# Nineteen block products instead of twenty-one in a per-sample weight combination, and a new order of one iteration

## The chip, the cores and the metric

The kernel runs on one core of a Trainium2 chip. The metric is the device time of one execution in microseconds (us), the smaller the better. The kernel before takes 482.57 us, the median of three runs (482.04 to 482.87).

## The reference

The input is x (128 samples, 64 channels, 1024 positions, float32) and a style vector of 128 numbers for each sample. Four convolutions of width 3 follow one another, of the kinds same, upsample, same, downsample. Each sample has its own weights: the shared ones, multiplied by a scale for each input channel that comes from the style, and normalised for each output channel. The upsample and the downsample have a fixed blur [1, 3, 3, 1]. No nonlinearity stands between the layers.

```python
def _layer(x, style, w, b, mw, mb, typ):
    s = style @ mw.T + mb
    weight = SCALE * w * s[:, None, :, None]
    demod = lax.rsqrt(jnp.sum(weight * weight, axis=(2, 3)) + EPS)
    weight = weight * demod[:, :, None, None]
    if typ == 'same':
        out = jax.vmap(_conv_same)(x, weight) + b[None, :, None]
    elif typ == 'upsample':
        out = jax.vmap(_conv_up)(x, weight.transpose(0, 2, 1, 3)) + b[None, :, None]
        out = _blur(out, 2.0 * blur_k, (1, 1))
    elif typ == 'downsample':
        xb = _blur(x, blur_k, (2, 2))
        out = jax.vmap(_conv_down)(xb, weight) + b[None, :, None]
...
out = x
for i, typ in enumerate(('same', 'upsample', 'same', 'downsample')):
    out = _layer(out, style, weights[i], biases[i], mod_w[i], mod_b[i], typ)
return x + out
```

## The kernel before, in words

Since everything is linear, the kernel folds the four layers and the two blurs into one convolution for each sample, and applies that one to x. The rows near the two ends of the sequence don't fit the folded convolution; they are worked out apart for all samples at once (functions `ends0` to `ends3` and `rest0` to `rest3_bias`), a small step in some of the iterations, and leave in a transfer of their own (`out_ends`).

**Tiling.** Four samples form a quad; there are 32 quads (`NQ`). Two samples stand above one another in the 128 partitions (64 channels each), and the other two beside them. Every matmul is therefore a 64 x 64 tile of TensorE, and four of them (rows upper or lower, columns upper or lower) make one step. The profile counts two TensorE instructions for each float32 matmul of the code.

**Weights of a quad, in three combinations.** All products here are of blocks, 64 x 64 numbers for each sample. `scale3` makes the scaled weights of the last layer (`wd`). `stage1` (for most quads in two halves, `stage1_a` and `stage1_b`) multiplies in layer 2 and leaves `S`. `stage2` multiplies in the upsampling layer and the blurs and leaves `R`, seven blocks for each sample, called r0 to r6 here. For most quads a part of `stage2` is worked out an iteration early (`share`, which writes into free columns of the bank of a running convolution, and `share_copy`, which ScalarE copies over). `stage3` multiplies in layer 0 and leaves the folded weights `Wf`: three kinds of output position, three blocks each. Kind 0 uses the plain weights w, kind 1 w/3, kind 2 -2w (`w0s`). `stage3` is called in two parts: kinds 0 and 1 into one pair of PSUM banks, kind 2 into the same pair afterwards, each followed by two scaled copies on ScalarE into `Wf`. With three weight taps and seven blocks a kind takes seven block products, so the three kinds take 21.

**The convolution of a quad.** The three kinds are combined on VectorE into five sets of weights (`combine_a`, `combine_b`; tile `H`, which with `Wf` serves five products) and x into five inputs (`in04`, `in1`, `in2`, `in3`, tile `T`). `conv3`, `conv1`, `conv2`, `conv4` and `conv0` are the five products, each in three groups of 340 columns; conv4 writes to `Y`, the others to `psA`. `sum1` and `sum2` on VectorE put the results together, `output` on ScalarE scales them and adds the bias, and `store` sends them out.

**Order.** Nothing is scheduled by a planner: the kernel switches to manual scheduling, and each engine takes its instructions in the order in which the Python code writes them. The loop over q (line 1207) overlaps five quads. In iteration q it does, for TensorE: `stage2` of c = q+2, `conv4` of q, `stage3` part 0 of c, `conv3` of n = q+1, `stage3` part 1 of c, group 0 of `conv0` of q, group 0 of `conv1` of n, `stage1_a` of s = q+4, the other two groups of `conv1`, group 1 of `conv0`, `stage1_b`, `share`, group 2 of `conv0`, and `conv2` of n. The steps of the row ends stand in `EXTRA` and `SLOTS`, by iteration and place. Waits between engines are put in by the framework where one instruction touches a tile that another engine reads or writes.

**PSUM.** The pool `ps_w` has one pair of banks, used in turn by `psS`, `psR`, `psW` and, for the row ends, `psE`; `ps_conv` has two pairs for `psA`, `ps_y` one for `Y`.

Of the kernel before, what the change touches and what calls it, by code (L numbers as in the profile page):

```python
# [48 lines left out]
F32 = mybir.dt.float32  # L49
# [5 lines left out]
C = 64  # L55
K = 3
# [7 lines left out]
def kernel(  # L64
# [9 lines left out]
    nc = tc.nc  # L74
    NP, P, NXC = x.shape
    B = 2 * NP
    NQ = B // 4
# [3 lines left out]
    HALF = (T, Bo)  # L81

    nc_v, nc_a, nc_g = nc.vector, nc.scalar, nc.gpsimd
# [3 lines left out]
    const = ctx.enter_context(tc.tile_pool(name="const", bufs=1))  # L87
    setup = ctx.enter_context(tc.tile_pool(name="setup", bufs=2))
    wd_pool = ctx.enter_context(tc.tile_pool(name="wd_pool", bufs=4))
    s_pool = ctx.enter_context(tc.tile_pool(name="s_pool", bufs=4))  # L90
    r_pool = ctx.enter_context(tc.tile_pool(name="r_pool", bufs=4))
    wf_pool = ctx.enter_context(tc.tile_pool(name="wf_pool", bufs=3))
    tpool = ctx.enter_context(tc.tile_pool(name="tpool", bufs=2))
    mpool = ctx.enter_context(tc.tile_pool(name="mpool", bufs=1))
# [3 lines left out]
    ps_w = ctx.enter_context(tc.tile_pool(name="ps_w", bufs=1, space=PSUM))  # L98
# [35 lines left out]
    woi = {2: weights(cuts[1] + KC), 0: weights(cuts[2] + 2 * KC), 1: weights(cuts[2] + 3 * KC)}  # L134
# [12 lines left out]

    one = const.tile([P, 1], F32, name="one")
    eps = const.tile([P, 1], F32, name="eps")
    Z = const.tile([P, 512], F32, name="Z")  # L150
    E = const.tile([P, NT, C], F32, name="E")
    w1s = const.tile([P, K + 1, K, C], F32, name="w1s")
    nc_v.memset(one, 1.0)
# [40 lines left out]
    wsq = const.tile([P, NL, K, C], F32, name="wsq")  # L194
# [70 lines left out]
    def var_newton(bs, ls=slice(0, NL)):  # L265
# [90 lines left out]
    Wq = {}  # L356
    chain = {}

    def scaled_copy(eng, dst, src, f):
        if eng is nc_a:  # L360
            nc_a.activation(dst, src, AF.Copy, scale=f)  # L361
        else:
            eng.tensor_scalar(dst, src, f, None, op0=ALU.mult)
# [39 lines left out]
    def flat(t):  # L403
        return t.rearrange("c a o -> c (a o)")
# [43 lines left out]
        whole[q] = t  # L448

    whole, shared_ps = {}, {}  # L450
    Ed = const.tile([P, 6, C], F32, name="Ed")

    def tap_differences():

# [66 lines left out]
    def stage2(q, pool=None, engs=(nc_a, nc_a), between=None):  # L521
        st = chain[q]
        shared = q in shared_ps
        ps = stage2_rest(q) if shared else unit(pool or ps_w, f"psR{q}")
        for n, e in enumerate(() if shared else (-2, -1, 0, 1, 2, 3, 4, 5, 6)):
            if e % 2 == 0:
                a, lo, m = slice(1, 4), e // 2 + 1, 3
            else:
                a, lo, m = slice(4, 6), (e + 3) // 2, 2
            for r, rows in enumerate(HALF):  # L530
                for c, cols in enumerate(HALF):
                    src = st[c if r == 0 else 1 - c]
# [10 lines left out]
        rt = []  # L543
        for r in range(2):
            t = r_pool.tile([P, 7, C], F32, tag="R", name=f"R{q}_{r}")
            scaled_copy(
                engs[r], t.rearrange("c t o -> c (t o)"), ps[r][:, : 7 * C], tC[:, q, r : r + 1]
            )
            rt.append(t)
        chain[q] = rt  # L550
        return ps

    def stage3(q, part, pool=None, engs=(nc_a, nc_a)):

        rt = chain[q]
        ps = unit(pool or ps_w, f"psW{q}_{part}")
        if part == 0:
            Wq[q] = (
                wf_pool.tile([P, 2, K, K, C], F32, tag="Wf", name=f"Wf{q}"),
                wf_pool.tile([P, 3, 2, K, C], F32, tag="H", name=f"H{q}"),  # L560
            )
        W = Wq[q][0]
        kinds = ((0, 1), (2,))[part]
        n = 0
        for i, kind in enumerate(kinds):
            for k in range(K):
                gs = [g for g in range(K) if 0 <= K * g + kind - k < 7]
                lo, m = gs[0], len(gs)
                first = K * lo + kind - k
                n += 1  # L570
                for r, rows in enumerate(HALF):
                    for c, cols in enumerate(HALF):
                        at = (K * i + lo) * C
                        nc.tensor.matmul(  # L574
                            ps[r][cols, at : at + m * C],
                            w0s[kind][rows, k, :],
                            rt[c][rows, first : first + K * (m - 1) + 1 : K, :],
                            start=(n == 1),
                            stop=(n == K * len(kinds)),
                            skip_group_check=True,  # L580
                        )
        for r in range(2):
            dst = W[:, r, kinds[0] : kinds[-1] + 1].rearrange("c t g o -> c (t g o)")
            scaled_copy(engs[r], dst, ps[r][:, : len(kinds) * K * C], t0[:, q, r : r + 1])
        return ps

    def residual(q):

        W = Wq[q][0]
        for r in range(2):  # L590
            v = W[:, r, 1, 1, :]
# [4 lines left out]

    def taps(q):
        W, H_ = Wq[q]
        return *(W[:, :, i] for i in range(K)), *(H_[:, i] for i in range(3))

    def combine_a(q):

# [71 lines left out]
    def product(q, m, ps, groups=range(K)):  # L674

        W, H_ = Wq[q]
        tag, i = SLOT[m]
        for g in groups:
            for s, rows in enumerate(HALF):
                for c, cols in enumerate(HALF):  # L680
                    if m in (0, 4):
                        w = W[rows, c, m // 2, g, :]
                    else:
                        w = H_[rows, m - 1, c, g, :]
                    nc.tensor.matmul(  # L685
                        ps[s][cols, :NB],
                        w,
                        Ts[q, tag][rows, c, i, g : g + NB],
                        start=(g == 0 and m == 3),
                        stop=(g == K - 1),  # L690
                        skip_group_check=True,
                    )
# [26 lines left out]
    def conv1(q, *groups):  # L719
        product(q, 1, banks(q), groups or range(K))  # L720
# [19 lines left out]
    def conv0(q, *groups):  # L740
        product(q, 0, banks(q), groups)
# [294 lines left out]
    first = PART[0]  # L1036
# [125 lines left out]


    EXTRA = {
        (1, 1): lambda: small_rest(1),
        (2, 1): lambda: (small_rest(2), var_root(REST, Y[:, 0])),
        (2, 2): lambda: (table_B(REST), table_Bn(REST), vector_a1(REST)),
        (3, 0): lambda: var_newton(*layers(2, 3)),
# [20 lines left out]
        (22, 0): lambda: (blur_side(0, 0), blur_side(1, 0)),  # L1189
        (23, 0): lambda: (blur_side(0, 1), blur_side(1, 1)),  # L1190
        (24, 0): lambda: (blur_side(0, 2), blur_side(1, 2)),
        (28, 1): rest3,
        (28, 2): rest3_bias,
    }

    def extra(*at):
# [6 lines left out]

    def late(q):
        return AHEAD <= q < NQ - 2

    for q in range(NQ):
        n, c, s = q + 1, q + 2, q + 3 + (q >= AHEAD)
# [20 lines left out]
        if n < NQ - 1:  # L1229
            if q == 0:  # L1230
                in_g01(n)
            if q == 1:
                in_g2(n)
                load(n + NX)
            combine_a(n)
            combine_b(n)
            if q == 0:
                in_g2(n)
                load(n + NX)
# [38 lines left out]
        if late(q):  # L1278
            for i in range(2):
                store(q, i, slice(2, K))  # L1280
            if late(q - 1):
                for i in range(3):
                    load(c + 1, slice(i, i + 1))
        if c < NQ:
            stage3(c, 0)
        conv3(n)
        copy_m3(n)
# [3 lines left out]
        if q in SMALL:  # L1291
            l, bs = SMALL[q]
# [3 lines left out]
            in3(c)  # L1296
        if q > 1:
            in_g01(c)
        if c < NQ:
            stage3(c, 1)  # L1300
        if q in SLOTS:
            slot(*SLOTS[q], Y_banks)
        if s < NQ:
            conv0(q, 0)
        if q in SMALL:
            small(q)
        if q == 2:
# [144 lines left out]
```

## Time and profile before

| | us |
|---|---|
| median of three runs | 482.57 |
| the profiled execution | 482.28 |
| its span, first to last instruction | 480.4 |
| TensorE busy | 472.2 (98%) |
| VectorE busy | 399.0 (83%) |
| ScalarE busy | 303.8 (63%) |
| one iteration of the steady middle (349.47 to 363.41) | 13.94 |

The profile is of one execution. PE is TensorE, PEld its weight loads, DVE VectorE, ACT ScalarE, POOL GpSimd, SP the queue that issues most transfers. A row of the groups names line, engine and operation, then output tile and inputs, shapes and count; behind the bars stand busy time, mean length of one, and the engine's idle time ahead of them with what ended it. A row of the timeline gives start, length, and how many instructions were merged into it, with idle time ahead of it in brackets. In the chain of waits a step of TensorE begins where the step before it ended. Line 685 is the matmul of the convolutions, 574 that of `stage3`, 467 those of `share` and the remaining `stage2`, 533 the full `stage2`, 390 `stage1`; line 361 holds all scaled copies on ScalarE, line 753 the outputs.

### The profile page before, as it was taken

What the parts mean: (1) busy time and instruction counts of PE and PEld (TensorE: products, weight loads), DVE (VectorE), ACT (ScalarE), POOL (GpSimd) and SP (SyncE); (2) the same over time, 40 slices, a digit from 0 to 9 for tenths busy, and PEclk for the clock granted to TensorE, in tenths of its full rate; (3) what the DMA queues carried; (4) which work ended last, traced back from release to release, by engine and by line L of the source; (5) the groups of instructions that cost most, each with busy time, mean ns of one, the idle gap of its engine ahead of it and who ended that gap; (6) DMA issues with size and microseconds to landing.
All of it is one profiled execution on the core that took longest, in us unless ns stands there. A gap on an engine that the chain in (4) does not pass through costs nothing.

```text
span 480.4 us, 25778 instructions
## 1 busy us (share of the span) xinstructions
PE 472.2 (98%) x11592; PEld 369.2 (77%) x11592; DVE 399.0 (83%) x660; ACT 303.8 (63%) x620; POOL 138.9 (29%) x171
## 2 busy tenths in 40 slices
PE   8999999999999999999999999999999999999995
PEld 7977787888788777878777798767777887877762
DVE  4899998799898888878868898758988887777984
ACT  5466666666667666766666666667666666665442
POOL 2533032635413333302333212333112333322100
PEclk9999999999999999999999999999999999999998
DMA  7116364245555346544445545345544445554314
GB/s 243 53 63 194 118 195 191 92 149 172 164 159 149 115 138 180 163 136 140 141 137 178 150 150 145 125 148 161 165 142 129 151 150 180 169 157 151 106 60 175
DMA packets 50494, 70.65 MB, mean 147 GB/s; under 512 B 5648, under 2 KB 47312, under 8 KB 50384
## 3 DMA queue, kind: packets, MB, share of 16 engines
q1 hardware_dynamic: 49792, 68.32, 44.7%
q8 instruction: 91, 1.49, 1.3%
q10 hardware_dynamic: 592, 0.69, 0.4%
q14 instruction: 19, 0.16, 0.1%
HBM read 35.36 MB, written 33.62 MB: 144 GB/s over the span
## 4 chain that ended last, share of the span: by engine, by line
PE 97%; DVE 2%; issue 0%; ACT 0%; ACTq 0%; DVEq 0%
PE psA L685 45%; PE psW L574 15%; PE Y L685 11%; PE psR L467 10%; PE psS L390 6%; PE psR L533 4%; PE psA L467 2%; PE Y L921 2%; PE Y L337 1%; PE Y L181 1%; DVE Oe L1011 0%; PE psM L205 0%; DVE o L755 0%; DVE y L595 0%; PE psE L921 0%
## 5 line engine op out<-in xcount | busy, mean ns | idle before, releaser
L685 PE MATMUL psA<-T,H 64*64 64x340 f32 x2304 | 193.3, 446 | 1.2 <-DVE y L595 0.9
L685 PEld LDWEIGHTS psA<-T,H 64*64 64x64 f32 x2304 | 100.2, 133 | 46.6 <-issue 3.3
L446 POOL TENSOR_TENSOR S<-S 128x128 f32<-128x128 f32 x28 | 15.0, 536 | 268.7 <-ACT S L361 261.5
L595 DVE SCALAR_TENSOR_TENSOR G<-X 128x684 f32<-128x684 f32 (+1 forms) x65 | 76.2, 1207 | 0.0
L685 PE MATMUL psA<-T,Wf 64*64 64x340 f32 x768 | 74.8, 446 | 0.0
L361 ACT ACTIVATE R<-psR,tC 128x448 f32<-128x448 f32 x63 | 36.5, 630 | 43.4 <-PE psR L467 26.8
L361 ACT ACTIVATE Wf<-psW,t 128x384 f32<-128x384 f32 (+1 forms) x126 | 56.3, 497 | 11.1 <-PE psW L574 10.8
L685 PE MATMUL Y<-T,Wf 64*64 64x340 f32 x768 | 62.9, 447 | 0.2 <-issue 0.2
L574 PE MATMUL psW<-R,w0s 64*64 64x128 f32 (+1 forms) x1536 | 63.1, 287 | 0.0
L574 PEld LDWEIGHTS psW<-R,w0s 64*64 64x64 f32 x1536 | 53.2, 133 | 5.9
L595 DVE SCALAR_TENSOR_TENSOR Y<-m,psA 128x680 f32<-128x680 f32 x32 | 27.8, 870 | 33.3 <-PE psA L685 33.3
L663 POOL TENSOR_TENSOR T<-G 128x684 f32<-128x684 f32 x28 | 50.9, 1817 | 0.0
L467 PE MATMUL psR<-S,E 64*64 64x64 f32 (+1 forms) x1536 | 50.6, 237 | 0.2 <-issue 0.2
L672 DVE TENSOR_TENSOR T<-G 128x1368 f32<-128x1368 f32 (+1 forms) x33 | 50.6, 1536 | 0.0
L658 POOL TENSOR_TENSOR T<-G 128x684 f32<-128x684 f32 x28 | 46.5, 1660 | 13.1 <-DVE G L595 13.1
L753 ACT ACTIVATE o<-Y,tb,td 128x340 f32<-128x340 f32 x63 | 36.6, 630 | 19.3 <-PE Y L685 16.7
L467 PEld LDWEIGHTS psR<-S,E 64*64 64x64 f32 x1536 | 43.2, 134 | 5.1 <-issue 0.3
L595 DVE SCALAR_TENSOR_TENSOR y<-psA,m 128x680 f32<-128x680 f32 x32 | 27.7, 865 | 23.1 <-PE psA L685 20.6
L390 PEld LDWEIGHTS psS<-wd,w2n 64*64 64x64 f32 x1120 | 38.3, 133 | 9.5
L685 PEld LDWEIGHTS Y<-T,Wf 64*64 64x64 f32 x768 | 32.9, 133 | 13.9 <-issue 1.1
L753 ACT ACTIVATE o<-psA,tb,td 128x340 f32<-128x340 f32 x63 | 37.0, 644 | 8.0 <-PE psA L685 8.0
L361 ACT ACTIVATE S<-psS,tBn 128x256 f32<-128x256 f32 x56 | 23.5, 470 | 28.2 <-PE psS L390 28.2
(153 smaller groups left out, 703.6 us busy)
## 6 DMA issues: line engine op xcount, KB each, us to landing
out<-o SPq DMA_DIRECT2D x167, 170.0 KB, 2.7
X<-in_x SPq DMA_DIRECT2D x150, 172.0 KB, 3.5
X<-in_x SPq DMA_DIRECT2D x14, 516.0 KB, 4.9
out<-o SPq DMA_DIRECT2D x6, 510.0 KB, 5.6
out<-o SPq DMA_DIRECT2D x2, 340.0 KB, 2.7
Xe<-in_x_ends SPq DMA_DIRECT2D x1, 512.0 KB, 6.5
out<-o ACTq DMA_DIRECT2D x3, 170.0 KB, 3.1
par<-in_params SPq DMA_DIRECT2D x2, 192.0 KB, 3.3
```

Source lines behind the costliest of these rows:

```text
L361: nc_a.activation(dst, src, AF.Copy, scale=f)
L390: nc.tensor.matmul(ps[r][cols, at * C : (at + n) * C], weight[rows], wd[c if r == 0 else 1 - c][rows, taps], start=first, stop=last, skip_ ...
L446: nc_g.tensor_add(t[:, :, 2], t[:, :, 2], t[:, :, 0])
L467: nc.tensor.matmul(dst[r][cols], weight[rows], st[c if r == 0 else 1 - c][rows, slots, :], start=False, stop=last, skip_group_check=True,)
L533: nc.tensor.matmul(ps[r][cols, lo * C : (lo + m) * C], E[rows, e + 2, :], src[rows, a, :], start=(n == 0), stop=(n == 8), skip_group_check ...
L574: nc.tensor.matmul(ps[r][cols, at : at + m * C], w0s[kind][rows, k, :], rt[c][rows, first : first + K * (m - 1) + 1 : K, :], start=(n == 1 ...
L595: nc_v.scalar_tensor_tensor(out, x, f, y, op0=ALU.mult, op1=op)
L658: eng.tensor_add(t[:, :, 0, :NJ], plane(g, 2), plane(g, 1))
L663: eng.tensor_sub(t[:, :, 1, :NJ], plane(g, 2), plane(g, 1))
L672: nc_v.tensor_sub(t[:, pairs, :, :NJ], both(a, PL), both(b, 1))
L685: nc.tensor.matmul(ps[s][cols, :NB], w, Ts[q, tag][rows, c, i, g : g + NB], start=(g == 0 and m == 3), stop=(g == K - 1), skip_group_check ...
L753: nc_a.activation(dst, src, AF.Identity, bias=add, scale=d3)
```

## The change

From quad 4 on (c = 4 to 31, 28 quads, the test `wide(q)`) the third combination is written anew. Kind 0 needs w0·r3 + w1·r2 + w2·r1 and kind 1 needs, over three, w0·r4 + w1·r3 + w2·r2 (and the same three blocks further on). Both hold w1 times one of two neighbours. With p = w1·(r2 + r3), kind 0 becomes p + w2·r1 + (w0 - w1)·r3 and kind 1 becomes p/3 + (w0/3)·r4 + ((w2 - w1)/3)·r2. So p is multiplied once and used twice; that takes 19 block products.

The new pieces: `r_sums` on VectorE makes the two sums and keeps them in `R`, whose tile grows from seven to nine blocks and holds both samples' halves; `tap_shares` on GpSimd makes the two weight differences, once; `stage3_b` does kind 2 and the first block of kind 0; `stage3_p` does p, and ScalarE writes p/3 from PSUM to PSUM beside it; `stage3_a` adds the rest. In `Wf` the kinds stand in another order (`KIND`), so that each of the two results is one run of blocks.

The order of a wide iteration changes too: `stage3_b` and `stage3_p` stand where part 0 stood, group 0 of `conv0` goes ahead of `stage3_a`, the three groups of `conv1` stand together ahead of `stage1_a`, and groups 1 and 2 of `conv0` together ahead of `stage1_b`. The two last steps of the row ends are called later, `rest3` at place 2 of iteration 28 and `rest3_bias` at place 0 of iteration 29. The weight differences `Ed` and `Wd` take over the space of `wsq`, and the constant `Z` has 384 columns.

```diff
-    r_pool = ctx.enter_context(tc.tile_pool(name="r_pool", bufs=4))
+    r_pool = ctx.enter_context(tc.tile_pool(name="r_pool", bufs=2))
-    Z = const.tile([P, 512], F32, name="Z")
+    Z = const.tile([P, 384], F32, name="Z")
-    Ed = const.tile([P, 6, C], F32, name="Ed")
+    later = wsq.rearrange("c l k o -> c (l k) o")
+    Ed = later[:, :6]
...
+    def tap_shares():
+        nc_g.tensor_sub(Wd[:, 0], woi[0][:, 0, :], woi[0][:, 1, :])
+        nc_g.tensor_sub(Wd[:, 1], w0s[1][:, 2, :], w0s[1][:, 1, :])
...
+    def same_row(ps, at, n, weight, t, slots, first=False, last=False):
+        for r, rows in enumerate(HALF):
+            for c, cols in enumerate(HALF):
+                nc.tensor.matmul(
+                    ps[r][cols, at * C : (at + n) * C],
+                    weight[rows],
+                    t[rows, c, slots, :],
+                    start=first,
+                    stop=last,
+                    skip_group_check=True,
+                )
...
+    def r_sums(q):
+        t = chain[q]
+        nc_v.tensor_add(t[:, :, 7:9], t[:, :, 2:6:3], t[:, :, 3:7:3])
+
+    def stage3_out(q, ps, at, i, j):
+        W = Wq[q][0]
+        for r in range(2):
+            dst = W[:, r].rearrange("c t g o -> c (t g) o")[:, i:j]
             scaled_copy(
+                nc_a, flat(dst), ps[r][:, at * C : (at + j - i) * C], t0[:, q, r : r + 1]
             )
+
+    def stage3_b(q):
+
+        new_w(q)
+        t = chain[q]
+        ps = wide_ps[q] = unit(ps_w, f"psW{q}")
+        same_row(ps, 3, 3, w0s[2][:, 2, :], t, slice(0, 7, 3), first=True)
+        same_row(ps, 3, 2, w0s[2][:, 1, :], t, slice(1, 5, 3))
+        same_row(ps, 3, 2, w0s[2][:, 0, :], t, slice(2, 6, 3))
+        same_row(ps, 6, 1, w0s[0][:, 0, :], t, slice(0, 1), last=True)
+        stage3_out(q, ps, 3, 0, 4)
+
+    def stage3_p(q):
+
+        ps, t = wide_ps[q], chain[q]
+        same_row(ps, 0, 2, w0s[0][:, 1, :], t, slice(7, 9))
+        for r in range(2):
+            scaled_copy(nc_a, ps[r][:, 3 * C : 5 * C], ps[r][:, : 2 * C], 1.0 / 3.0)
+
+    def stage3_a(q):
+
+        ps, t = wide_ps.pop(q), chain[q]
+        same_row(ps, 2, 2, w0s[1][:, 0, :], t, slice(1, 5, 3))
+        same_row(ps, 2, 1, w0s[1][:, 1, :], t, slice(0, 1))
+        same_row(ps, 0, 2, w0s[0][:, 2, :], t, slice(1, 5, 3))
+        same_row(ps, 0, 2, Wd[:, 0], t, slice(3, 7, 3))
+        same_row(ps, 3, 2, Wd[:, 1], t, slice(2, 6, 3), last=True)
+        stage3_out(q, ps, 0, 4, 9)
...
-        (28, 1): rest3,
-        (28, 2): rest3_bias,
+        (28, 2): rest3,
+        (29, 0): rest3_bias,
...
+    def wide(q):
+        return 2 <= q < NQ - 2
...
-            combine_b(n)
+            if wide(q):
+                combine_b(n, (0,))
+                r_sums(c)
+                combine_b(n, (1, 2))
+            else:
+                combine_b(n)
...
-        if c < NQ:
+        if wide(q):
+            stage3_b(c)
+            stage3_p(c)
+        else:
             stage3(c, 0)
         conv3(n)
...
-        if c < NQ:
+        if wide(q):
+            conv0(q, 0)
+            stage3_a(c)
+        else:
             stage3(c, 1)
         if q in SLOTS:
             slot(*SLOTS[q], Y_banks)
-        if s < NQ:
+        if not wide(q):
             conv0(q, 0)
...
-        conv1(n, 0)
+        conv1(n, *(range(K) if wide(q) else (0,)))
         if twice:
             stage1(s - 1)
         elif s < NQ:
             stage1_a(s)
         elif q == NQ - 4:
             slot(ends3, 3, unit(ps_w, "psE"), 3)
-        conv1(n, 1, 2)
+        if not wide(q):
+            conv1(n, 1, 2)
...
-        conv0(q, *((1,) if s < NQ else (0, 1)))
+        conv0(q, *((1, 2) if wide(q) else (1,)))
...
-        conv0(q, 2)
+        if not wide(q):
+            conv0(q, 2)
```

More of the change, by code (lines that the diff above doesn't have):

```diff
@@ L542, in stage2 @@
             between()
-        rt = []
+        t = r_pool.tile([P, 2, 9, C], F32, tag="R", name=f"R{q}")
         for r in range(2):
-            t = r_pool.tile([P, 7, C], F32, tag="R", name=f"R{q}_{r}")
+            scaled_copy(engs[r], flat(t[:, r, :7]), ps[r][:, : 7 * C], tC[:, q, r : r + 1])
+        chain[q] = t
+        return ps
+    KIND = {0: 1, 1: 2, 2: 0}
+    Wd = later[:, 6:8]
+    def tap_shares():
+        nc_g.tensor_sub(Wd[:, 0], woi[0][:, 0, :], woi[0][:, 1, :])
+        nc_g.tensor_sub(Wd[:, 1], w0s[1][:, 2, :], w0s[1][:, 1, :])
@@ new lines, in new_w @@
+    def new_w(q):
+        Wq[q] = (
+            wf_pool.tile([P, 2, K, K, C], F32, tag="Wf", name=f"Wf{q}"),
+            wf_pool.tile([P, 3, 2, K, C], F32, tag="H", name=f"H{q}"),
+        )
[9 more added lines that the diff above has]
+                    skip_group_check=True,
+                )
@@ L546, in stage2 @@
+    wide_ps = {}
+    def r_sums(q):
[5 more added lines that the diff above has]
+            dst = W[:, r].rearrange("c t g o -> c (t g) o")[:, i:j]
             scaled_copy(
-                engs[r], t.rearrange("c t o -> c (t o)"), ps[r][:, : 7 * C], tC[:, q, r : r + 1]
+                nc_a, flat(dst), ps[r][:, at * C : (at + j - i) * C], t0[:, q, r : r + 1]
@@ L548, in stage2 @@
             )
-            rt.append(t)
-        chain[q] = rt
-        return ps
+    def stage3_b(q):
[7 more added lines that the diff above has]
+        stage3_out(q, ps, 3, 0, 4)
@@ L557, in stage3 @@
         if part == 0:
[L558 to L561, printed above, removed]
+            new_w(q)
         W = Wq[q][0]
@@ L576, in stage3 @@
                             w0s[kind][rows, k, :],
-                            rt[c][rows, first : first + K * (m - 1) + 1 : K, :],
+                            rt[rows, c, first : first + K * (m - 1) + 1 : K, :],
                             start=(n == 1),
@@ L582, in stage3 @@
         for r in range(2):
-            dst = W[:, r, kinds[0] : kinds[-1] + 1].rearrange("c t g o -> c (t g o)")
+            at = KIND[kinds[0]]
+            dst = W[:, r, at : at + len(kinds)].rearrange("c t g o -> c (t g o)")
             scaled_copy(engs[r], dst, ps[r][:, : len(kinds) * K * C], t0[:, q, r : r + 1])
@@ L590, in residual @@
         for r in range(2):
-            v = W[:, r, 1, 1, :]
+            v = W[:, r, KIND[1], 1, :]
             nc_v.scalar_tensor_tensor(v, idn3, t3[:, q, r : r + 1], v, op0=ALU.mult, op1=ALU.add)
@@ L598, in taps @@
         W, H_ = Wq[q]
-        return *(W[:, :, i] for i in range(K)), *(H_[:, i] for i in range(3))
+        return *(W[:, :, KIND[i]] for i in range(K)), *(H_[:, i] for i in range(3))
     def combine_a(q):
@@ L681, in product @@
                     if m in (0, 4):
-                        w = W[rows, c, m // 2, g, :]
+                        w = W[rows, c, KIND[m // 2], g, :]
                     else:
@@ L1164 @@
     EXTRA = {
-        (1, 1): lambda: small_rest(1),
+        (1, 1): lambda: (small_rest(1), tap_shares()),
         (2, 1): lambda: (small_rest(2), var_root(REST, Y[:, 0])),
```

## The prediction

> **What bounds the kernel now.** I read the page first: shares, slices, chain.
>
> ```profile
> span 480.4 us, 25778 instructions
> PE 472.2 (98%) x11592; PEld 369.2 (77%) x11592; DVE 399.0 (83%) x660; ACT 303.8 (63%) x620; POOL 138.9 (29%) x171
> ...
> PEclk9999999999999999999999999999999999999998
> ...
> PE 97%; DVE 2%; issue 0%; ACT 0%; ACTq 0%; DVEq 0%
> ```
>
> TensorE bounds the kernel from end to end: 97% of the chain, at full granted clock. So a matmul column saved is time saved, and any wait put in TensorE's queue is time lost, since nothing else stands in that queue to fill it. Next, one iteration in the chain of waits, a steady one (start, length, step):
>
> ```profile
> 349.47 1.94 PE psR L467 x112
> 351.41 1.72 PE Y L685 x24
> 353.13 1.52 PE psW L574 x48
> 354.65 1.72 PE psA L685 x24
> 356.37 0.76 PE psW L574 x24
> 357.13 1.14 PE psA L685 x16
> 358.27 0.55 PE psS L390 x24
> 358.82 1.72 PE psA L685 x24
> 360.54 0.23 PE psS L390 x16
> 360.77 0.35 PE psA L467 x24
> ```
>
> The steps touch without a gap; the next iteration starts at 363.41, after 13.94 us. They are stage2, conv4, stage3 part 0 (at 353.13), conv3, stage3 part 1 (356.37), and so on. Then the timeline of the other engines around the two psW steps and later in the iteration:
>
> ```profile
> 352.55 0.55 DVE L595 SCALAR_TENSOR_TENSOR H<-Wf 128x384 f32<-128x384 f32 x1
> ...
> 353.14 0.56 DVE L595 SCALAR_TENSOR_TENSOR H<-Wf,H 128x384 f32<-128x384 f32 x1
> 353.20 1.16 ACT L753 ACTIVATE o<-Y,tb,td 128x340 f32<-128x340 f32 x2 [0.53 <-PE Y L685]
> ...
> 354.69 1.05 ACT L361 ACTIVATE Wf<-psW,t 128x384 f32<-128x384 f32 x2 [0.33 <-PE psW L574]
> ...
> 358.92 0.84 ACT L361 ACTIVATE S<-psS,tBn 128x256 f32<-128x256 f32 x2 [1.02 <-PE psS L390]
> ...
> 360.89 0.60 DVE L443 SCALAR_TENSOR_TENSOR S<-psS,tB,S 128x128 f32<-128x128 f32 x2
> 361.59 0.81 DVE L462 TENSOR_TENSOR S<-S 128x256 f32<-128x256 f32 x1
> 361.76 0.63 ACT L490 COPY psR<-psA 128x256 f32<-128x256 f32 x2 [0.89 <-PE psA L685]
> ...
> 362.29 1.18 ACT L753 ACTIVATE o<-psA,tb,td 128x340 f32<-128x340 f32 x2
> ...
> 363.34 1.03 ACT L361 ACTIVATE wd<-w3x,tA 128x320 f32<-128x320 f32 x2
> ```
>
> After conv4 ends at 353.13 ScalarE does the two outputs from `Y`, then the two copies of psW, 0.04 us after part 0 ends (354.65 to 354.69). TensorE meanwhile does conv3, so the copies cost nothing.
>
> **The change part by part.**
>
> *Matmul columns.* The psS steps price a matmul by width: 16 of 64 columns take 0.23 us (14.4 ns each); 16 of 128 and 8 of 64 take 0.55, so 128 columns take (0.55 - 0.115)/16 = 27.2 ns. Part 0 (16 of 192, 32 of 128) takes 1.52, so 192 take (1.52 - 0.87)/16 = 40.6 ns. Price goes with columns; more, narrower instructions cost nearly nothing. New: `stage3_b` has 8 instructions each of 192, 128, 128, 64 columns: 8 x 109.4 ns = 0.875 us. `stage3_p`: 8 x 27.2 = 0.218. `stage3_a`: 8 x (4 x 27.2 + 14.4) = 0.986. Sum 2.08 against 1.52 + 0.76 = 2.28: 0.20 us saved a quad, 5.6 over 28 quads.
>
> *The wait of `stage3_p`.* It writes columns 0 to 127 of the banks from which ScalarE has just begun to copy columns 192 to 447 (`stage3_out` of `stage3_b`). Its columns are free; its bank is not. In the built program of the changed kernel (here quad 13; TensorE, then ScalarE) there is a wait:
>
> ```
> L566 Matmult psW13_0_3627<-R13_3589,par_97 64x128 [waits DVE_49,Activation_49]
> L566 Matmult psW13_1_3628<-R13_3589,par_97 64x128 [waits Activation_49]
> L747 Matmult psA12_3653<-T3_12_3408,H12_3362 64x340 x12
> ...
> L815 Activation o11_3614<-Y_124,tb_142,td_141 128x340 x2
> L361 Activation Wf13_3625<-psW13_0_3627,t0_139 128x256 [waits PE_49]
> L361 Activation Wf13_3625<-psW13_1_3628,t0_139 128x256 [waits PE_49]
> ```
>
> The counts that the two matmuls wait for are those which the two `Wf` copies raise, r = 0 and r = 1. The trace has the like: the copy L490 reads columns of `share`, yet waits for conv0 beside them in the same bank (psA L685, not L467):
>
> ```profile
> L490 ACT COPY psR<-psA 128x256 f32<-128x256 f32 x48 | 15.2, 361 | 22.0 <-PE psA L685 21.0 <-DVE S L443 1.0
> L361 ACT ACTIVATE S<-psS,tBn 128x256 f32<-128x256 f32 x56 | 23.5, 470 | 28.2 <-PE psS L390 28.2
> L462 DVE TENSOR_TENSOR S<-S 128x256 f32<-128x256 f32 x24 | 15.2, 632 | 2.4
> L457 POOL TENSOR_TENSOR Ed<-E 128x128 f32<-128x128 f32 x2 | 1.4, 701 | 0.0
> ```
>
> The Trainium skill says so too (PSUM — Partial Sum Buffer, section "PSUM bank collisions raise a hardware error"): guard PSUM by bank and quadrant, not by address, because two engines in one bank collide even at disjoint columns. By that rule the sum is the 511 below, by columns alone 476; row L490 agrees with the rule.
>
> The price. `stage3_b` ends at 353.13 + 0.875 = 354.005. ScalarE is still in the `Y` outputs: a third instruction starts 1.05 to 1.06 us after the first of a pair (362.29 to 363.34), so at 353.20 + 1.06 = 354.26. Two copies of 256 columns take 0.84 (358.92): until 355.10. From a release to TensorE's next start:
>
> ```profile
> 441.33 0.73 ACT L361 ACTIVATE Wf<-psW,t 128x192 f32<-128x192 f32 x2
> ...
> 441.80 1.43 PEld L921 LDWEIGHTS psE<-Ue,par 64*64 64x64 f32 x24 [0.16 <-ACT Wf L361]
> L361 ACT ACTIVATE Wf<-psW,t 128x192 f32<-128x192 f32 x63 | 23.1, 417 | 0.6 <-PE psW L574 0.4 <-PE Y L841 0.2
> L574 PE MATMUL psW<-R,w0s 64*64 64x128 f32 x1024 | 49.3, 269 | 0.0
> ```
>
> The first copy ended at 441.33 + 0.417 = 441.75, the load began at 441.80: 0.05. With 0.01 to the matmul, 0.27 for the matmul itself (269 ns, which a stream overlaps) and three more at 0.027, `stage3_p` ends at 355.10 + 0.06 + 0.27 + 0.08 = 355.51. Unhindered it would end at 354.005 + 0.218 = 354.22. The stall is 1.29 us, and behind it in TensorE's queue stand conv3 and the whole rest of the iteration. ScalarE and VectorE are waiting for TensorE then, and nobody makes it up: 28 x 1.29 = 36.1 us.
>
> Bounds: were ScalarE free when `stage3_b` ends (354.05), all comes 0.21 earlier: 1.08 a quad, 30.2. Did its instructions not overlap at all (353.20 + 1.16 + 2 x 0.47 = 355.30), 0.20 later: 1.49, 41.7. I take the middle, which goes by the overlaps that the trace shows.
>
> *`r_sums`.* 256 elements on VectorE, as L462: 0.63 (0.81 at worst). It starts one issue interval after 352.55, about 353.02, and ends by 353.65 to 353.83, ahead of 354.005 and far ahead of the copies: no cost. The two `H` operations behind it come 0.6 later, near 354.8, and conv1 needs them only after 357: no cost.
>
> *The p/3 copies.* Two on ScalarE, no longer than L490's 0.36 each, beside conv3 (1.72 us) and group 0 of conv0 (0.57) before `stage3_a` needs them. Without that cover 0.7 a quad.
>
> *The order.* `stage1_b` waits for the two S copies, which end at 358.92 + 0.84 = 359.76; 0.94 after `stage1_a` ends in the chain (358.82). Ahead of it now stand two groups of conv0, 1.14, where 1.72 stood. Cover remains, but by 0.2 in chain time and about nothing after restart: 0 to 0.1 a quad, 0 to 2.8 in all; I take 0. `share_copy` no longer waits for a group of conv0 but for L443's reads, later by some 0.4; stage2 needs it 1.72 after conv2 starts, and 0.6 remains. The early group 0 of conv0 needs nothing that isn't old.
>
> *Row ends.* At iteration 28 `rest3` stood ahead of sum1 (tile y) on VectorE, and conv2 waited for it:
>
> ```profile
> 444.01 2.37 DVE L1011 SCALAR_TENSOR_TENSOR Oe<-raw,dm 128x192 f32<-128x192 f32 x2 [1.40 <-ACT raw L776]
> ...
> 446.30 0.85 DVE L595 SCALAR_TENSOR_TENSOR y<-psA,m 128x680 f32<-128x680 f32 x1
> ...
> 447.30 1.95 PE L685 MATMUL psA<-T,H 64*64 64x340 f32 x24 [0.71 <-DVE y L595]
> ```
>
> Called later, it stands behind sum1, so the 0.71 goes. It is then ahead of sum2 of iteration 29; stage2 of quad 31 covers that. `out_ends` leaves some microseconds later, behind other stores on SP's queue and long before the end. Gain 0.7 us.
>
> *The rest.* `tap_shares` is two small GpSimd operations, once, as L457 (0.7 each, of twice the width), an iteration ahead of use. The R tiles hold as many quads as before. Smaller Z and shared space: nothing.
>
> *Sum.* -5.6 + 36.1 - 0.7 = +29.8. The profiled execution took 482.28 us, 0.29 under the median: 482.28 + 29.8 = 512.1 us. One steady iteration becomes 13.94 - 0.20 + 1.29 = 15.03. Ends by the bounds: -5.6 + 30.2 - 0.7 = 23.9, which is 506.2 (504.8 if the release took none of its 0.05); -5.6 + 41.7 - 0.7 + 2.8 = 38.2, with the row ends' gain lost too 38.9, which is 521.2.
>
> **The rivals.**
>
> *Faster: the wait is empty.* If `stage3_p` needn't wait for the copies, or they were over, only columns count: 482.28 - 5.6 - 0.7 = 476.0. For it: the columns are disjoint and 98% of the span is TensorE work. Against it: the waits in the built program, row L490, and that the copies can't start before 354.05 while `stage3_p` is due at 354.005. It decides from a stall under 6.3/28 = 0.225 us a quad; the lowest bound is 1.03. Chance 0.06.
>
> *No change: `r_sums` is the wait.* With the bank free, `stage3_p` would still need the sums. A VectorE late by 0.2 to 0.25 us past 354.005, so done at 354.2, would eat the gain: 482 us. By the rows it is done by 353.83 at worst, and this needs the first rival's free bank besides. Chance 0.02.
>
> *The clock falls with the gaps.* Two rows of stretches (start and end, length, busy time of the five engines with counts, granted clock, DMA share, GB/s):
>
> ```profile
> 440.00:448.00 8.00, 7.18 (x116) 5.54 (x112) 6.59 (x8) 4.28 (x9) 3.38 (x2) 1.00 0.57 178
> ...
> 472.00:480.00 8.00, 3.31 (x48) 1.51 (x40) 2.44 (x5) 2.22 (x4) 0.00 (x0) 0.87 0.51 176
> ```
>
> With 0.82 us of 8 idle the clock stayed whole; with 4.7 of 8 it fell to 0.87. At 0.87 all through, 28 iterations of 13.74 us of matmuls would gain 28 x 2.05 = 57 us: 569. The new gap is 1.29 of 15, like the first row. Chance 0.02. The Trainium skill (TensorE: Matmul & The Clock Gate, section "A second HAM failure mode: psum-queue depth-cycling") tells of a kernel whose short idles between groups of matmuls made the clock swing; the row of 440 to 448 speaks against it here.
>
> *More is uncovered*: `stage1_b` or a ScalarE step that now stands late adds over 0.1 a quad: above 521. Chance 0.02.
>
> **How the numbers follow.** The wait as priced has 0.88, and I predict its 512.1. The range, 505 to 521, is that case's own bounds; 0.12 lies outside. A measurement of this kernel tells about 0.2% (1 us) from no change. Faster 0.06, same 0.02, slower 0.92.
>
> **What would show it.** Right: a steady iteration near 15.0 us; TensorE idle some 1.3 us in it, ahead of the 128-column psW steps of `stage3_p`, the releaser being ScalarE's `Wf` copy of 256 columns; the chain of waits crossing from TensorE to ScalarE there, ScalarE's share of the chain a few per cent instead of 0; the psW matmuls of a wide quad 2.08 us net of the gap; the clock still 1.0. Each step wrong: the gap ended by `r_sums` (VectorE too late), psW work of 2.2 or more (narrow matmuls not priced by columns), a gap ahead of `stage1_b` or stage2 (cover gone), a clock under 1.0. The prediction is wrong if iterations are shorter than 13.94, which needs the gap under 0.2.

## The result, and the profile after

| | before | after |
|---|---|---|
| median (lowest to highest, 5 runs each) | 482.32 us (481.89 to 482.87) | 515.45 us (515.34 to 517.3) |
| ratio | | 1.0695, 95% interval 1.0675 to 1.0715 |
| profiled execution: time, span | 482.28, 480.4 us | 515.38, 513.6 us |
| a steady iteration | 13.94 us | 15.07 us |

The change makes the kernel 33 us slower. The forecast was 512.1 us, in a range of 505 to 521. The lengths of iterations, here and below, are read from the trace as the time from one start of conv4 to the next.

The page of the changed kernel, the lines that answer to those shown of before: instructions, shares, clock, and the chain that ended last by engine.

```profile
span 513.6 us, 26449 instructions
PE 484.4 (94%) x11816; PEld 404.2 (79%) x11816; DVE 418.8 (82%) x688; ACT 314.1 (61%) x676; POOL 139.4 (27%) x173
...
PEclk9999999999999999999999999999999999999999
...
PE 81%; ACT 8%; issue 6%; POOL 3%; DVE 1%; ACTq 0%; DVEq 0%; POOLq 0%
```

TensorE's share of the chain falls from 97 to 81%, and ScalarE, which held nothing of it, has 8%. Of the 6% of "issue", 21 us are two early pieces (from 62.48 and 77.77), where the chain runs over GpSimd; from 200 us on it is under 1%. The clock is whole. Where the chain passes to ScalarE is seen in the chain of waits of one steady iteration (start, length, step):

```profile
377.10 1.74 PE Y L747 x22
378.84 0.02 issue
378.86 1.16 ACT o L815 x2
380.03 0.38 ACT Wf L361
380.40 0.04 issue
380.44 0.69 PE psW L566 x6
381.14 0.10 PE psA L747
```

Conv4 (`Y`) releases ScalarE's two outputs, these hold up the first `Wf` copy, and 0.04 us after that copy ends TensorE begins `stage3_p`. The same place in the timeline, the rows that matter (the bracket at the end of a line is the idle time before it and what ended it):

```profile
378.34 0.42 DVE L579 TENSOR_TENSOR R<-R 128x256 f32<-128x256 f32 x1
378.55 1.02 PE L566 MATMUL psW<-R,w0s 64*64 64x192 f32 x23
...
378.86 1.16 ACT L815 ACTIVATE o<-Y,tb,td 128x340 f32<-128x340 f32 x2 [0.58 <-PE Y L747]
...
379.92 0.84 ACT L361 ACTIVATE Wf<-psW,t 128x256 f32<-128x256 f32 x2
...
380.44 0.69 PE L566 MATMUL psW<-R,par 64*64 64x128 f32 x6 [0.75 <-ACT Wf L361]
...
380.81 0.14 PEld L566 LDWEIGHTS psW<-R,par 64*64 64x64 f32 x2 [0.17 <-ACT Wf L361]
...
380.99 0.63 ACT L361 ACTIVATE psW<-psW 128x128 f32<-128x128 f32 x2 [0.23 <-PE psW L566]
```

The sums (L579) are over at 378.76, 1.6 us ahead of `stage3_p`, so it isn't the sums that it waits for. The waits, summed up (us in all, times, longest), and the group of the `stage3_b` and `stage3_p` matmuls:

```profile
PEld psW L566 <- ACT Wf L361: 29.8, 55, 1.1
PE psW L566 <- ACT Wf L361: 20.4, 27, 0.8
PE psW L566 <- DVE R L579: 0.9, 1, 0.9
PEld psS L390 <- ACT S L361: 0.9, 2, 0.7
PEld psR L468 <- issue: 1.8, 7, 0.4
L566 PE MATMUL psW<-R,par 64*64 64x128 f32 (+1 forms) x672 | 50.1, 261 | 21.4 <-ACT Wf L361 20.4
```

The first two lines are the bank wait, 27 and 55 times over 28 quads: the matmul's idle time and that of the weight load ahead of it, which overlap and are not to be added. The other three are small, and are what the forecast did not have: sums that came late once, `stage1_b` held up by the S copies, and gaps in stage2 that nothing in the trace releases.

### The profile page after: what moved, and what is told of

It is laid out like the page before. It is cut to its first block, busy times and chain, and to the rows that moved or that the text cites. A ratio compares the mean times of both kernels' runs of the same rounds, so it can differ in the third digit from the quotient of the medians.

```text
span 513.6 us, 26449 instructions
## 1 busy us (share of the span) xinstructions
PE 484.4 (94%) x11816; PEld 404.2 (79%) x11816; DVE 418.8 (82%) x688; ACT 314.1 (61%) x676; POOL 139.4 (27%) x173
## 3 DMA queue, kind: packets, MB, share of 16 engines
q8 instruction: 92, 1.51, 1.3%
## 4 chain that ended last, share of the span: by engine, by line
PE 81%; ACT 8%; issue 6%; POOL 3%; DVE 1%; ACTq 0%; DVEq 0%; POOLq 0%
PE psA L747 39%; PE Y L747 10%; PE psR L468 9%; PE psW L566 9%; ACT o L815 6%; PE psS L390 6%; PE psR L534 2%; ACT Wf L361 2%; PE psW L635 2%; PE Y L983 2%; PE psA L468 1%; POOL T L725 1%; POOL T L720 1%; PE Y L337 0%; PE Y L181 0%
## 5 line engine op out<-in xcount | busy, mean ns | idle before, releaser
L747 PE MATMUL psA<-T,H 64*64 64x340 f32 x2304 | 197.4, 447 | 0.2 <-DVE y L657 0.2
L747 PEld LDWEIGHTS psA<-T,H 64*64 64x64 f32 x2304 | 120.0, 133 | 28.3 <-DVE y L657 1.6
L566 PE MATMUL psW<-R,par 64*64 64x128 f32 (+1 forms) x672 | 50.1, 261 | 21.4 <-ACT Wf L361 20.4
L361 ACT ACTIVATE Wf<-psW,t 128x256 f32<-128x256 f32 (+3 forms) x126 | 56.3, 500 | 22.2 <-PE psW L566 19.2
L566 PEld LDWEIGHTS psW<-R,par 64*64 64x64 f32 x672 | 32.3, 133 | 29.9 <-ACT Wf L361 29.8
L468 PEld LDWEIGHTS psR<-S,E 64*64 64x64 f32 x1536 | 50.9, 134 | 3.1 <-issue 1.4
L779 ACT COPY m<-psA 128x680 f32<-128x680 f32 x32 | 23.3, 727 | 43.3 <-PE psA L747 43.3
L566 PE MATMUL psW<-R,w0s 64*64 64x128 f32 (+2 forms) x1120 | 49.4, 269 | 0.0
L390 PEld LDWEIGHTS psS<-wd,w2n 64*64 64x64 f32 x1120 | 42.7, 133 | 7.1 <-ACT S L361 0.9
L747 PEld LDWEIGHTS psA<-T,Wf 64*64 64x64 f32 x768 | 40.5, 133 | 9.8
```

The costliest lines, as they stand in the source:

```text
L390: nc.tensor.matmul(ps[r][cols, at * C : (at + n) * C], weight[rows], wd[c if r == 0 else 1 - c][rows, taps], start=first, stop=last, skip_ ...
L468: nc.tensor.matmul(dst[r][cols], weight[rows], st[c if r == 0 else 1 - c][rows, slots, :], start=False, stop=last, skip_group_check=True,)
L566: nc.tensor.matmul(ps[r][cols, at * C : (at + n) * C], weight[rows], t[rows, c, slots, :], start=first, stop=last, skip_group_check=True,)
L747: nc.tensor.matmul(ps[s][cols, :NB], w, Ts[q, tag][rows, c, i, g : g + NB], start=(g == 0 and m == 3), stop=(g == K - 1), skip_group_check ...
L779: nc_a.copy(m3c[q][:, s], a)
```

## The experiments

All of them give the whole result; none leaves work out. The time of the kernel before, beside the first four, was 482.13 us; beside the last four 481.88.

**The wait taken away.** `stage3_out` is called behind the matmuls of `stage3_p`, so that the copies still share the bank but nothing waits for them.

```diff
 def stage3_b(q):
-    stage3_out(q, ps, 3, 0, 4)
 def stage3_p(q):
     same_row(ps, 0, 2, w0s[0][:, 1, :], t, slice(7, 9))
+    stage3_out(q, ps, 3, 0, 4)
```

> Edit: the matmuls of stage3_p are issued ahead of the copies of stage3_out, so that they stand ahead of ScalarE's reads of the bank; all else as changed. Theory (stage3_p waits for the bank that ScalarE copies from): the 1.29 us gap of each wide quad goes, and what is left is the saving, 476 to 477 us, a steady iteration of 13.75 us. Rival A (VectorE's sums are the wait): the gap stays, above 510. Rival B (the new order or the narrow products themselves cost): part stays, 485 to 505. The measured time was 3.3 us above the forecast; if that part belongs to the order, this comes out near 479.

Measured: 483.27 us, ratio 1.0019 (1.0004 to 1.0035). 32 us of the 33 are gone with one line moved, and the first lines of the table of waits show that the gap went too:

```profile
PE Y L181 <- DVE eps L156: 1.4, 1, 1.4
PE psW L566 <- DVE R L579: 1.3, 2, 0.9
PE psR L468 <- issue: 0.9, 3, 0.4
```

The wait for the copies of its bank is the cause. But the time is not the 476 to 477 that columns alone would give. Undisturbed iterations do take 13.74 us, 0.20 under 13.94, just as priced; the gain is lost in others: iteration 2 takes 1.06 us more than before and iteration 6 0.66, with gaps in front of `stage3_p` that VectorE's sums end (the second line); iterations 3 and 5 take 0.53 and 0.48 more, as in the next experiment; and several have gaps of 0.26 to 0.59 us in stage2 (psR).

**The order alone.** The 21 products and both parts of `stage3` as before, in the changed kernel's order, with its row ends.

```diff
-        if wide(q):
-            stage3_b(c)
-            stage3_p(c)
-        else:
-            stage3(c, 0)
+        stage3(c, 0)
```

(and so for part 1, with no sums)

> Edit: the 21 products of before, in two parts, inside the changed order of the iteration (conv0 group 0 ahead of part 1, conv1 whole, conv0 groups 1 and 2 together, row ends later); no sums. Theory: the order costs nothing and the row ends give 0.7 us, 481.5 to 482; if the cover of stage1_b is short by up to 0.1 us a quad, up to 484.5. Rival B (the order is what costs): over 490.

Measured: 483.22 us, ratio 1.002 (1.0005 to 1.0036). Steady iterations take 13.94, as before, so the order costs nothing there. In iteration 3, the one with two `stage1`, it costs 0.74 us: the third group of conv0, which stood between its second `stage1_a` and `stage1_b`, now stands ahead of both, and `stage1_b` starts 0.58 us after the matmul ahead of it, when the S copies let it. Iteration 28 gets 1.37 shorter by the row ends. Iteration 5 loses 0.57 at its end, where conv4 of iteration 6 waits for VectorE's sum into `Y` (two timelines, VectorE and TensorE):

```profile
117.51 1.43 DVE L920 SCALAR_TENSOR_TENSOR cc<-b1s,cc 128x96 f32<-128x96 f32 x1
118.86 0.86 DVE L657 SCALAR_TENSOR_TENSOR Y<-m,psA 128x680 f32<-128x680 f32 x1
```

```profile
119.77 1.66 PE L747 MATMUL Y<-T,Wf 64*64 64x340 f32 x20 [0.38 <-DVE Y L657]
```

L920 belongs to the row ends and stands ahead of that sum in the kernel before, too; there the sum was over at 118.94 and conv4 began at 119.08, so the cover was 0.14 us. In the new order the operations on `S` ahead of them end later.

**The wait made longer.** The copy of the second bank is made twice, in the same place.

```diff
 def stage3_b(q):
      stage3_out(q, ps, 3, 0, 4)
+    dst = Wq[q][0][:, 1].rearrange("c t g o -> c (t g) o")[:, 0:4]
+    scaled_copy(nc_a, flat(dst), ps[1][:, 3 * C : 7 * C], t0[:, q, 1:2])
```

> Edit: the second of the two copies that follow stage3_b is made twice (same values, 28 more copies of 128x256). Theory: those copies stand in the path of TensorE, so each adds the 0.37 us by which ScalarE starts instructions behind one another: 28 x 0.37 = 10.4, 525.9 us. Rivals A and B: ScalarE has 39% to spare, no change, 515.4.

Measured: 529.08 us, ratio 1.0971 (1.0951 to 1.0992). Per quad 13.6 / 28 = 0.49 us are added, not 0.37. The timeline says why: the three copies take 1.35, against 0.84 for two above, so one more costs 0.51 and not the usual interval between ScalarE's instructions.

```profile
388.90 1.17 ACT L817 ACTIVATE o<-Y,tb,td 128x340 f32<-128x340 f32 x2 [0.57 <-PE Y L749]
389.95 1.35 ACT L361 ACTIVATE Wf<-psW,t 128x256 f32<-128x256 f32 x3
```

TensorE pays for a longer copy in full (steady iterations take 15.58 instead of 15.07): what ScalarE holds of the bank is on the path.

**The sums later.** `r_sums` behind the whole of `combine_b` instead of behind its first operation.

```diff
-                combine_b(n, (0,))
+                combine_b(n)
                 r_sums(c)
-                combine_b(n, (1, 2))
```

> Edit: VectorE makes the sums behind all of combine_b instead of between its steps, about 1.0 us later. Theory: they are then done about 0.2 us before ScalarE's second copy is over, so nothing changes, 515 to 517. Rival A (the sums end the wait): 28 x 1.0 = 28 us more, about 543.

Measured: 519.18 us, ratio 1.0763 (1.0745 to 1.078), 2 us above the range expected. Steady iterations keep their 15.07 us and the releaser stays ScalarE's copy; the sums are not the wait there. What comes on top comes early on, where VectorE is late as it is: iteration 2 takes 2.8 us more than in the changed kernel, 6 takes 0.4 more, with the two VectorE lines below; later iterations differ to both sides by the gaps in stage2.

```profile
PE psW L566 <- ACT Wf L361: 19.1, 25, 0.9
PE psW L566 <- DVE Y L1365: 2.9, 2, 2.1
PE psW L566 <- DVE R L579: 1.7, 1, 1.7
```

**What stands ahead of the copies.** `stage3_b` with its copies is called ahead of the two outputs from `Y`.

```diff
+        if wide(q):
+            stage3_b(c)
         for i in range(2):
             output(q, 2, i)
...
         if wide(q):
-            stage3_b(c)
             stage3_p(c)
```

> The changed kernel, with ScalarE's two Y outputs (plane 2) issued behind stage3_b and its two Wf copies instead of ahead of them; stage3_p's matmuls still wait for both Wf copies. Theory (the p matmuls wait for two Wf copies which themselves stand on ScalarE behind the Y outputs): the copies then begin when stage3_b's last matmul has ended, about 0.2 us earlier than now, so each gap gets shorter by about 0.2 us: 515.4 - 0.2 x 28 = about 509.8 us. Rival (the wait is set by the length of the copies alone, or by a wait of TensorE that has nothing to do with ScalarE's order): 515.4 unchanged.

Measured: 510.12 us, ratio 1.0585 (1.0565 to 1.0604), 5.3 us under the changed kernel; steady iterations 14.80 instead of 15.07. ScalarE's copies now start as `stage3_b` ends, and the outputs follow:

```profile
375.33 0.84 ACT L361 ACTIVATE Wf<-psW,t 128x256 f32<-128x256 f32 x2 [1.38 <-PE psW L566]
376.06 1.16 ACT L815 ACTIVATE o<-Y,tb,td 128x340 f32<-128x340 f32 x2
```

So of the stall some 0.2 to 0.27 us is ScalarE's queue, and the rest the copies themselves.

**The row ends alone.** The kernel before, with only its two last operations of the row ends moved.

```diff
-        (28, 1): rest3,
-        (28, 2): rest3_bias,
+        (28, 2): rest3,
+        (29, 0): rest3_bias,
```

> The kernel before, with only the row ends' last operations moved (rest3 to (28,2), rest3_bias to (29,0)). Prediction's term: -0.7 us (481.4 from 482.1); the trace of the changed kernel lost gaps of 0.42 and 1.16 us there, by which it would be -1.5 (480.6). Rival: 482.1, unchanged, if the gaps come back elsewhere.

Measured: 481.0 us, ratio 0.9984 (0.9972 to 0.9997): 0.8 us faster. Iteration 28 gets 1.03 us shorter. The second experiment has this gain too, and so the order alone costs the difference of the two ratios: 0.0036 of the time, 1.7 us, give or take 1 by the intervals.

**The gaps in stage2.** They come late in psR or among the conv4 matmuls behind it, with no releaser. Their lengths here are from one matmul's start to the next. When all TensorE matmuls of the trace are counted from the start, those of the first experiment's kernel, which has no bank wait, lie at counts that are 85, 81, 80, 78, 75, 74, 73 and 70 modulo 128, in iterations 4, 9, 10, 12, 15, 16, 17 and 20, whatever the matmul there does. Before has three such (iterations 17, 19 and 27, 0.32, 0.67 and 0.38 us, counts 73, 72 and 63; the second is in conv4). 128 matmuls and their weight loads are 256 instructions, and the page of the changed kernel, with as many matmuls, has queue 8 bring 92 packets (packets, MB, share of the engines' time) for 11816 of each, some 128 of each to a packet:

```profile
q8 instruction: 92, 1.51, 1.3%
```

To tell the place in the stream from the place in the work, zeros were added to the zeroing of `Y` at the start, which moves everything behind them along the stream.

```diff
     zeros_to_y(2, 96, False)
+    zeros_to_y(40, 2, False)
```

> The kernel with the copies behind stage3_p's matmuls (e1_copies_behind_p, 483.27), with 80 matmuls of 2 columns of zeros added to the zeroing of Y at the start, where TensorE waits for data. Nothing else changes; every later instruction of TensorE's stream lies 160 instructions further on, so the boundaries of the packets in which its instructions are fetched fall 80 matmuls earlier in the program. Theory (the unexplained gaps of 0.14 to 0.59 us in psR's stage, always at the same place modulo 128 matmuls, are TensorE waiting for its next packet of instructions, in the stage where 128 matmuls go by in 3.5 us): the gaps in psR go, about -3.3 us, 480 us (with the added matmuls up to +1). Rival (something in the work itself, its data or its order): the gaps stay in the same iterations and at the same matmuls of psR, 483.3 to 484.

Measured: 484.72 us, ratio 1.0054 (1.0039 to 1.0069); the time forecast failed, for two reasons that the timeline shows. The first line is the shifted kernel, the second (of the last experiment) one without the zeros:

```profile
1.36 6.04 PE L181 MATMUL Y<-Z 64*64 64x384 f32 x176 [1.36 <-DVE eps L156]
```

```profile
1.36 1.88 PE L181 MATMUL Y<-Z 64*64 64x384 f32 x16 [1.36 <-DVE eps L156]
```

The 80 instructions are 160 matmuls in the trace, so the stream moved by 160 - 128 = 32 places, not 80; and they are not hidden but take 4 us. The first conv4 starts at 34.7 us; in the profiled execution without the zeros it is 33.4, and in the eight other kernels 31.2 to 32.2. From there to the last conv4 the profiled execution is 1.9 us shorter than without the zeros (438.1 against 440.1). The places answer the question: the gaps late in psR of iterations 4, 9, 10, 12 and 15 to 17 are gone, and new ones stand in 20, 21, 24 and 25, at counts of 70, 69, 66 and 65 modulo 128. That is the same slowly falling series at other matmuls: in iteration 20, which has a gap both ways, it moved from matmul 110 of psR's 112 to matmul 78, by just the 32 of the shift. (One gap of 0.50 in iteration 5, at 120, isn't part of it: it is the wait for the sum into `Y` of the second experiment.) In the shifted kernel, stage2 at the end of iteration 25 and of iteration 17 (which has a gap of 0.51 without the shift) differ so; first the psR line that begins stage2, then the lines around its end:

```profile
407.91 0.49 PE L468 MATMUL psR<-S,E 64*64 64x128 f32 x8
...
409.85 0.45 PE L747 MATMUL Y<-T,Wf 64*64 64x340 f32 x1
409.89 0.22 PE L468 MATMUL psR<-S,E 64*64 64x64 f32 x2
410.42 0.80 PE L747 MATMUL Y<-T,Wf 64*64 64x340 f32 x8
```

```profile
293.86 0.43 PE L468 MATMUL psR<-S,E 64*64 64x128 f32 x8
...
295.79 1.93 PE L747 MATMUL Y<-T,Wf 64*64 64x340 f32 x24
```

From the first psR matmul to conv4 running freely it is 2.5 us against 1.93, and the difference is the step from 409.89 to 410.42. The place of these gaps goes by the instruction stream, not by the work: shown.

What TensorE waits for there can be read from the times of the single packets of queue 8, which the traces hold. The ten traces together have 47 such gaps (steps of over 0.2 us in psR, of over 0.48 among conv4's matmuls, which otherwise start up to 0.3 apart). Each lies within one matmul of a series that has a place every 127.7 matmuls (127.5 in the four kernels with the bank wait), and one packet comes in for each place. The matmul behind a gap starts 1.2 to 1.6 us after its packet has come in: the one at 410.42 after a packet that was in at 409.08. From count 2000 on, the series has 769 places in the ten traces, and at all but one (1.1 us) the matmul starts 1.2 us or more after its packet, gap or not. So the times fit a wait for the packet of instructions: where TensorE comes to the place sooner, as in stage2, which does 112 matmuls in 1.94 us (128 would take 2.2, not the 3.5 of the expectation), it stands until then. No run changed a packet's time, and what sets the start of a packet stays open.

Which of the late places show a gap also changes from one execution to the next: the kernel with only the row ends moved has before's matmuls up to iteration 28, yet no gap in iterations 17 and 19, but one in 26. So part of the differences between single profiles is chance.

**Both repairs.** As the first experiment, and the new products and order only from iteration 7 (quad 9) on, past the iterations with late sums and two `stage1`.

```diff
     def wide(q):
-        return 2 <= q < NQ - 2
+        return 7 <= q < NQ - 2
```

> As e1_copies_behind_p (copies behind stage3_p's matmuls), with the new products and the new order only from iteration 7 on (quad 9) instead of iteration 2 (quad 4). Theory: the late sums of iterations 2 and 6 (gaps of 1.07 and 0.66 us) and the stall of iteration 3 (0.58 us) go, 23 quads save 0.20 us each, the row ends 0.7 to 1.5: 482.1 - 4.6 - 0.7 to 1.5 = 476 to 477 if the fetched packets' gaps stay away (its stream is 40 matmuls shorter up to there, which puts the packets' boundaries outside psR), 479 if they do not. Rival (the gain of 0.20 us is eaten by the new order itself in every stretch): 482 to 483.

Measured: 475.56 us, ratio 0.987 (0.9852 to 0.9887), 6.3 us faster than before, 40 faster than the change, and just under the 476 to 477 expected where the gaps stay away. Iterations 3 to 6 are as long as before, and nearly all steady ones from 7 take 13.74. The waits that remain after the start (the first line, which before has too) are small:

```profile
PE Y L181 <- DVE eps L156: 1.4, 1, 1.4
PE psA L747 <- DVE y L657: 0.6, 2, 0.4
PE psR L468 <- issue: 0.4, 1, 0.4
```

Here TensorE runs from `stage3_b` (the 192-column line and part of the next) through `stage3_p` into conv3 with no gap, 1.10 us from 349.77 to 350.87, while ScalarE comes to the copies behind:

```profile
349.77 0.99 PE L566 MATMUL psW<-R,w0s 64*64 64x192 f32 x24
350.53 0.56 PE L566 MATMUL psW<-R,par 64*64 64x64 f32 x16
350.87 1.94 PE L747 MATMUL psA<-T,H 64*64 64x340 f32 x24
```

```profile
350.04 1.16 ACT L815 ACTIVATE o<-Y,tb,td 128x340 f32<-128x340 f32 x2 [0.54 <-PE Y L747]
351.10 0.84 ACT L361 ACTIVATE Wf<-psW,t 128x256 f32<-128x256 f32 x2
351.83 0.44 ACT L361 ACTIVATE psW<-psW 128x128 f32<-128x128 f32 x2
```

In this kernel the series of counts falls into the last third of psR in no iteration from 4 on, and stage2 has one gap left (iteration 22, 0.66 us, count 68, at matmul 36 of psR).

## Why the prediction was right

- *Columns, -0.20 a quad*: right. Without the wait steady iterations take 13.74 instead of 13.94, and `stage3_b` with `stage3_p` takes 1.10 where 0.875 + 0.218 = 1.09 was worked out. Narrower, more numerous matmuls did cost by their columns.
- *The bank wait, +1.29 a quad*: right in place, cause and size. Steady iterations grew by 1.13, which with the 0.20 saved makes a stall of 1.33. Taking the copies out of the way took 32 us off, making one longer added all of its length, and taking the `Y` outputs from ahead of them gave back 5.3 us where the lower bound, a free ScalarE, had 0.21 x 28 = 5.9. One detail was different: the first bank's matmuls start after the first copy, not after both; the second bank's wait for the second (their weight load at 380.81, 0.05 us after the two copies end). The 511 that the prediction names beside the rule on banks is a slip: its own sum gives 512.1.
- *`r_sums` at 0*: right in steady iterations, where moving them later changes nothing. Wrong in iteration 2, where VectorE is late: 0.9 us. The prediction worked it out from one steady iteration and let it stand for all.
- *The order at 0 (0 to 0.1 a quad)*: the sum, 1.7 us, is within the bounds, but the picture was wrong. It is not a little in each quad: steady ones lose nothing, iteration 3 loses 0.74, iteration 5 0.57 to the sum into `Y`, and most of the rest is gaps in stage2. The prediction looked for the order's cost in `stage1_b` of a steady iteration, and not at the row ends' work that stands ahead of that sum.
- *Row ends, -0.7*: 0.8 alone (0.1 to 1.3 by the interval). In the changed kernel the idle time that y's sum ended ahead of conv2 is 0.2, where it was 0.71 at this place alone:

```profile
L747 PE MATMUL psA<-T,H 64*64 64x340 f32 x2304 | 197.4, 447 | 0.2 <-DVE y L657 0.2
```

- *The clock*: it stayed whole, with 1.3 us idle in 15. That rival is out.
- *The 3.3 us by which the profiled execution is above the forecast* are the terms of the early iterations (3 to 6 lie 0.3 to 0.6 us each above the 1.09 forecast, 9 and 12 by 0.8 and 0.6), 0.04 us of stall a quad (1.1 in all) and the gaps in stage2 and conv4, which 9 and 12 have too. Iteration 19 and the row ends give back 0.6 and 0.8; iteration 19 because it has a gap in the profile of before (count 72) and none here. Iteration 5 ends on VectorE's sum into `Y` here as well: the sum is over at 124.53 and conv4 begins at 124.58. In iteration 4 the changed kernel has a gap of 0.28 in stage2, and in two others (the first and the shifted experiment) conv2 starts 0.3 us late behind VectorE's sum y; with the `Y` outputs moved behind the copies, iteration 4 loses nothing beyond a steady one. How much of 3 to 6 each of these makes was not measured singly.
- *The faster rival's 476.0* was worked out for a stall of nothing. The first experiment, which has no stall, took 483.3: the rival's sum left out the same things. Only where those are avoided too, in the last kernel, does a time of that size, 475.6, come out.

## What to carry to other kernels

In this program the waits went by PSUM bank and not by columns, although the columns were disjoint. So before splitting a group of matmuls so that one part is copied out while another is still to be written, look at which copy stands between them in the built program, and issue the later matmuls ahead of the copy. On an engine that is busy from end to end a stall's price is its length times its count, while a gain of a few tenths an iteration is real only in iterations whose other engines keep up; look at the first iterations and the odd ones by themselves, and leave the change out there. An experiment that removes the suspected wait and nothing else shows both the cause and what the change would have been worth.

## What the runs showed of the hardware that was not expected

- Short gaps in stage2, 0.2 to 0.67 us each, at places 127.5 to 127.7 matmuls apart in the instruction stream, in a stage that takes 17 ns a matmul (1.94 us for 112). The matmul behind each of 47 gaps started 1.2 to 1.6 us after a 16 KB packet (1.51 MB in 92) of queue 8 had come in. Adding 160 matmuls at the start moved the gaps to other iterations. In one execution they add up to single microseconds.
- A second copy with the same source and destination as the one just ahead of it cost 0.51 us of ScalarE's time, where the interval between two copies to different places was 0.84 - 0.47 = 0.37.
- The matmuls with 2 columns of zeros took (6.04 - 1.88) / 160 = 26 ns each at the start, more than the 14.4 ns of 64 columns in steady work; the rows there cover matmuls of other widths too, so the figure is rough.
